# Count groups of one or two nodes with src split 64 x 196 instead of 32 x 391, and group sizes chosen by new tables

## The chip, the cores and the metric

The kernel runs as one program on one core of a Trainium2 chip. The metric is the device time of one execution in microseconds (us), as the median over runs. One execution was also recorded by the hardware profiler; lines such as L920 are lines of the kernel before. The engines are called by the profile's names: PE (TensorE matmul), PEld (its weight load), DVE (VectorE), ACT (ScalarE), POOL (GpSimd) and SP (SyncE, which only issues DMAs).

## What is computed

A graph has 12500 nodes with 64 features and 400000 edges `src -> dst`, sorted by `dst`; `dst` is drawn as 12500 times the square of a uniform number, so nodes with low numbers have many more edges than those with high ones. `src` is uniform. Cut to what matters:

```
x_t  = leaky_relu(x @ W1n + b1n) @ W2n + b2n             # node MLP
e_t  = leaky_relu(ea @ W1e + b1e) @ W2e + b2e            # edge MLP
agg  = segment_sum(x_t[src] * e_t, dst)                  # messages
x    = layernorm(x + layernorm0(x + agg) * gamma + beta) # layer 0
deg  = number of edges with dst = node, plus 1
w    = rsqrt(deg)
h    = x
twice: h = w * (sum over edges (src, dst) of (w*h)[dst] into src  +  w*h)
out  = layernorm(x + h @ W.T + b)                        # layer 1
```

The two hops at the end need, for each pair of nodes, how many edges join them: the count matrix `A[dst, src]`.

## The kernel before

**Three kinds of work share the first 4.3 ms.**

*Messages.* Edges go through in 261 batches `q` of 1536 edges (12 chunks of 128), from the highest `dst` to the lowest. For each chunk POOL issues one indirect DMA (`gathers`, L592) that fetches the 128 rows `x_t[src]` into the tile `xg`; 3125 chunks give 3125 such DMAs. The edge MLP (`hidden`, L624 to L640, and `message`, L648 to L663) runs on PE, ACT and DVE; L659 multiplies by `xg`; `level1` and `level2` (L674 to L720) sum into PSUM by destination, and `nodes` finishes the layer for four windows of 128 nodes at a time. `xg` has four buffers.

*Counting* (`adjacency`, L875). The matrix `A` is made in blocks `k` of four destination nodes, 3125 of them, from the highest to the lowest. `src` is written as `a*391 + b` with 32 values of `a` (`FA`) and 391 of `b` (`FB`). A block's edges are cut into groups of `w` nodes (1, 2 or 4; with w = 8 one group serves two blocks) and a group into slots of at most 128 edges, in a number that depends on the expected count of edges alone (`_plan_slots`, L74). For each slot DVE makes a one-hot matrix of `b` (128 edges x 391, tile `oh`, L910), and for several slots at a time a one-hot of the key `node*32 + a` (tile `koh`, L859, 512 columns wide). One matmul (L920) of the two adds the slot's counts to `w*32` rows of a PSUM bank; with w = 8 there are two matmuls, one for each block. With w = 2 the two groups of a block use halves of 64 rows, with w = 1 four groups use quarters of 32 rows. ACT turns the finished bank into fp8 (`stage`, L935) and every eight blocks one DMA stores them to `adj` in HBM, in runs of 391 bytes. A row of `A` is 32*391 = 12512 columns long (`PITCH`).

The 44 table columns of 128 slots (`NSBP`, a multiple of four) are filled as follows: at the start 44 indirect DMAs (`run`, L320) find where each slot's edges begin, and later one indirect DMA per column (`fetch`, L799) brings the edges. `prepare` (L807, once per four columns, 11 times) computes key and column of every edge on DVE (L814 to L826), and four transposes each on PE spread them.

*First hop* (`hop1`). When a supergroup of rows of `A` has been stored and its nodes are done, PE multiplies it, in 25 pieces of 512 columns (the last of 224), with L1117 and L1129, and `combine` (L1246) adds the result up.

**What sets the order.** The main loop (L1331) has 264 steps `t`. In step `t` it emits the gathers of batch `t+2`, the edge MLP of batch `t`, the messages of `t-1` and so on, and between them as much counting and first hop as a budget says. `_plan_slots` gives each block a cost, `a_total` is their sum with 20 for each block (L1289), and by step `t` the share `(t + lead) / 261` of it is emitted (L1349), with `lead` growing from 1 to 10 over the first 60 steps. So a block's cost decides how many blocks fall into a step. The first hop gets 4400 units a step. The scheduler of the language then orders each engine's queue; the edge work has priority.

A gather also waits for the matmul that `marks` names (L600): the gather that stands nine places back in the queue waits for the matmul that was emitted last. So POOL can't run far ahead of PE.

When all counting is emitted (step 249) the counting buffers are freed, and `scatter_store` (L1083) prepares 27 batches for the second hop. After the last gather the last nodes are finished (L1199 to L1212), and the second hop begins: 24 pieces of 512 columns and one of 224, each with 80 matmuls of 128 rows (L1221) and 80 of 64 (L1232).

## Time and profile before

| | |
|---|---|
| median of 10 runs | 5064.64 us (5056.83 to 5073.96) |
| the profiled execution's own time | 5066.32 us |
| its span, first to last instruction | 5064.5 us |
| mean granted PE clock | 0.904 |
| busy, of the span | PE 86%, PEld 49%, DVE 65%, ACT 45%, POOL 75% |
| gathers (L592) | 3125, 1003 ns each, from 71 us to 4276 us |
| one-hots of columns (L910) | 5556, 334 ns each |
| one-hots of keys (L859) | 1170, about 420 ns each |
| counting matmuls (L920) | 6054 |
| evictions of count banks (L935, L933) | 3125 |

Busy shares say how long an engine had something in work, not whether anything waited for it. What sets the pace has to be read from the waits: an engine whose queue always has an instruction ready, and which starts it as soon as the one before has ended, sets the pace of its stage, whatever its busy share is. In a group's row, the mean is one instruction's own duration; where neighbours overlap, their sum is more than the busy time.

### The profile page before, as it was taken

The page shows a single profiled execution, that of the slowest core. Times are in us where ns is not written, and L with a number is a line of the kernel's source. Part 1 is how long each engine was busy: PE and PEld are TensorE (multiplying, and loading weights), DVE is VectorE, ACT ScalarE, POOL GpSimd, SP SyncE. Part 2 cuts the span into 40 slices and gives each one's busy share as a digit, 9 for nine tenths or more (in the row PEclk, how much of TensorE's full clock was granted, in tenths as well). Part 3 has the DMA queues.
Part 4 walks back from the last instruction along what each step waited for, and adds up shares of the span by engine and source line. Part 5 has one row for each costly group of instructions (what it writes and reads, how often), then busy time and mean ns, then how long its engine had stood idle before and what let it go on. Part 6 is the DMA issues. An engine that isn't in the chain of part 4 may idle for free. (4 is left out here: it accounts for less than half of the span.)

```text
span 5064.5 us, 94143 instructions
## 1 busy us (share of the span) xinstructions
PE 4357.3 (86%) x31344; PEld 2483.7 (49%) x31344; DVE 3267.4 (65%) x11086; ACT 2265.5 (45%) x7868; POOL 3804.5 (75%) x3607
## 2 busy tenths in 40 slices
PE   5776889989989898978897898698787978999997
PEld 3443445545545455544554455354444545444443
DVE  7897778766758786786688686766778856100004
ACT  3887777555545464554555443333332123100003
POOL 6777767777777777777777777777777765688885
PEclk8898999999999798979998899898789967999999
DMA  5998889766768586646674665454333253999998
GB/s 139 182 169 133 142 153 158 146 138 139 144 125 155 116 152 130 127 88 140 136 141 89 132 129 98 86 117 90 65 81 76 66 145 97 231 210 211 205 200 222
DMA packets 1254836, 696.96 MB, mean 138 GB/s; under 512 B 593468, under 2 KB 1188144, under 8 KB 1253312
## 3 DMA queue, kind: packets, MB, share of 16 engines
q1 hardware_dynamic: 1104032, 566.91, 49.1%
q0 software_dynamic: 150304, 123.92, 17.4%
q8 instruction: 248, 4.06, 0.4%
q14 instruction: 252, 2.06, 0.1%
HBM read 494.67 MB, written 195.83 MB: 136 GB/s over the span
## 5 line engine op out<-in xcount | busy, mean ns | idle before, releaser
L592 POOL DMA_INDIRECT xg<-xt_tab,si x3125 | 3134.5, 1003 | 1012.1 <-issue 492.8
L935 ACT ACTIVATE stage<-pa 128x391 fp8e4<-128x391 f32 x3077 | 1514.5, 538 | 1166.6 <-PE pa L920 1089.3
L910 DVE TENSOR_SCALAR oh<-iota_b,colT 128x391 bf16<-128x391 bf16 x5556 | 1605.7, 334 | 188.3 <-PE pa L920 183.5
L920 PE MATMUL pa<-oh,koh 128*128 128x391 bf16 (+2 forms) x6054 | 1303.2, 372 | 279.8 <-ACT stage L935 75.1
L920 PEld LDWEIGHTS <-koh 128*128 128x128 bf16 (+2 forms) x6054 | 607.5, 150 | 664.8 <-issue 371.2
L935 ACT ACTIVATION_READ_ACCUMULATOR stage<-pa 128x1 f32 x3077 | 734.7, 244 | 0.0
L1117 PE MATMUL hacc_p<-at,gp 128*128 128x512 fp8e4 (+1 forms) x2425 | 646.5, 396 | 96.0 <-ACT gp L744 36.6
L659 DVE TENSOR_TENSOR msg<-pe,xg 128x384 f32<-128x384 f32 x522 | 289.8, 555 | 594.0 <-DMA xg<-xt_tab,si 343.8
L1492 POOL DMA_INDIRECT hop_tab<-tot,first x317 | 493.7, 1558 | 100.5 <-issue 93.9
L650 PEld LDWEIGHTS pe<-w,z 128*128 128x128 f32 x3132 | 463.9, 209 | 73.5 <-issue 51.4
L650 PE MATMUL pe<-w,z 128*128 128x128 f32 x3132 | 475.3, 292 | 0.0
L1221 PE MATMUL acc<-at,gp 128*128 128x512 fp8e4 (+1 forms) x2000 | 446.2, 376 | 0.0
L1117 PEld LDWEIGHTS <-gp 128*128 128x128 bf16 x2425 | 231.7, 103 | 406.6 <-issue 162.9
L634 ACT ACTIVATE z<-pw,b1s 128x384 f32<-128x384 f32 x522 | 293.7, 617 | 211.3 <-PE pw L624 203.3
L624 PE MATMUL pw<-eat,w1ab 64*128 64x384 f32 x1044 | 372.5, 601 | 17.7 <-DVE msg L659 12.6
L859 DVE TENSOR_TENSOR koh<-iota_k,keyT 128x512 bf16<-128x512 bf16 (+3 forms) x920 | 384.6, 419 | 0.0
L1129 PE MATMUL hacc_p<-at,gp 128*64 128x512 fp8e4 (+1 forms) x2425 | 367.6, 391 | 0.0
L1600 DVE TENSOR_TENSOR pot<-po,dis 128x256 f32<-128x256 f32 (+2 forms) x26 | 10.5, 408 | 539.4 <-PE po L1594 539.4
L638 DVE SCALAR_TENSOR_TENSOR z<-pw,b,z 128x384 f32<-128x384 f32 x522 | 313.0, 607 | 39.0 <-ACT z L634 35.6
L1221 PEld LDWEIGHTS <-gp 128*128 128x128 bf16 x2000 | 188.2, 99 | 227.4 <-issue 29.0
L684 PE MATMUL pl<-msg,oh 128*32 128x65 f32 x6264 | 170.4, 232 | 127.7 <-DVE msg L659 119.3
L1246 PEld LDWEIGHTS pc<-twoid,hev 128*128 128x128 f32 x1764 | 235.6, 203 | 58.2 <-issue 27.7
(218 smaller groups left out, 3846.2 us busy)
## 6 DMA issues: line engine op xcount, KB each, us to landing
adj<-stage SPq DMA_DIRECT2D x390, 391.0 KB
at<-adj SPq DMA_DIRECT2D x97, 896.0 KB
at<-adj SPq DMA_DIRECT2D x168, 512.0 KB
eat<-in_eaq_dram SPq DMA_DIRECT2D x261, 192.0 KB
xg<-xt_tab,si POOLq DMA_INDIRECT x3125
at<-adj SPq DMA_DIRECT2D x96, 256.0 KB
at<-adj SPq DMA_DIRECT2D x24, 832.0 KB
at<-adj SPq DMA_DIRECT2D x24, 768.0 KB
```

Source lines behind the costliest of these rows:

```text
L592: got = nc.gpsimd.indirect_dma_start(out=xg[:, i, :], out_offset=None, in_=xt_tab, in_offset=bass.IndirectOffsetOnAxis(ap=si[:, c : c + 1] ...
L624: nc.tensor.matmul(pws[h], w1ab[rows, h, :], ea_q[rows], start=True, stop=True, tile_position=(D * h, 0),)
L638: nc.vector.scalar_tensor_tensor(z[:, h, :], pws[h], b1, z[:, h, :], op0=ALU.add, op1=ALU.max)
L650: ended = nc.tensor.matmul(pe[:, :, c, :], z[:, h, c * P : (c + 1) * P], w2, start=False, stop=(c == SCC - 1),)
L859: nc.vector.tensor_tensor(t[:, :, :n], iota_8[:, :, :n] if w == 8 else iota_k[:, : w * FA, :n], keyT[:, None, j0 : j0 + n].to_broadcast([P ...
L910: nc.vector.tensor_scalar(oh, iota_b, colT[:, i % P : i % P + 1], None, op0=ALU.is_equal)
L920: ended = nc.tensor.matmul(to, key, oh, start=(j == 0), stop=(j == caps[g] - 1), tile_position=(0, r0),)
L935: nc.scalar.activation(stage[:, u, :], pa, AF.Identity, saturate=True, accum_out=sums[:, u : u + 1],)
L1117: nc.tensor.matmul(acc[:, :w], gp[:kk, lo + i, 0:2, :].rearrange("p t d -> p (t d)"), t[:kk, i, :w], start=start, stop=False, skip_group_c ...
L1129: nc.tensor.matmul(acc[D * h : D * (h + 1), :w], gp[:kk, lo + i, 2, :], t[:kk, i, :w], start=False, stop=False, skip_group_check=True, til ...
L1221: nc.tensor.matmul(acc[:, :w], gp[:kk, wi, 0:2, :].rearrange("p t d -> p (t d)"), t[:kk, wi - lo, :w], start=first and n == 0, stop=False, ...
L1492: nc.gpsimd.indirect_dma_start(out=hop_tab[(q * QC + i) % HT], out_offset=bass.IndirectOffsetOnAxis(ap=first[:, q - Q0, i : i + 1], axis=0 ...
```

## The change

`FB` becomes 392, `FB2` 196. Groups of one or two nodes (w <= 2, called *halved*) write `src` as `a*196 + b` with 64 values of `a`. Their one-hot of `b` is 196 columns wide, their key is `node*64 + a`, so one slot takes 128 rows with w = 2 and 64 rows with w = 1, and two groups lie side by side in the two halves of a bank's columns. Their slots go group by group instead of by turns, and a dependency keeps their matmuls in that order on PE. A bank is stored in runs of 196 bytes, and a store holds blocks of one kind only. `PITCH` becomes 12544, so the last piece of a hop has 256 columns.

The sizes are chosen by a new table `value`, pairs of blocks with w = 8 are allowed everywhere, and a new table `cost` paces the loop; the empty block of a pair now has the cost 0. `prepare` multiplies by per-slot constants (`sQ`, `sA`, `sF`) where it used constants of the program, and these are made once at the start.

What follows from the two versions of `_plan_slots`, worked out from their formulas:

| | before | after |
|---|---|---|
| slots with w = 1 / 2 / 4 / 8 | 307 / 2389 / 2362 / 498 | 1394 / 2566 / 1401 / 498 |
| slots, counting matmuls | 5556, 6054 | 5859, 6357 |
| one-hots of keys | 1170 | 1425 |
| columns of slots `NSBP` | 44 | 48 |
| `a_total` | 1790922 | 1480492 |
| stores to `adj` | 391 | 394 |

Blocks 2046 and up (w = 4, one slot), 1548 to 2045 (w = 8) and 512 to 1547 (w = 2, two slots) keep their sizes; below 512 most blocks with w = 4 become w = 1.

```diff
-FB = 391
+FB = 392
+FB2 = FB // 2
 PITCH = FA * FB
-PAIR_END = 2304
...
-    cost = {1: 249, 2: 267, 4: 302}
+    cost = {1: 181, 2: 217, 4: 302, 8: 373}
+    value = {1: 51, 2: 61, 4: 82, 8: 109}
...
-            c = cost[w] * sum(caps)
+            c = value[w] * sum(caps)
...
-    for k in range(0, PAIR_END, 2):
+    for k in range(0, NBLK - 1, 2):
...
-        if 2 * n <= sum(blocks[k][2]) + sum(blocks[k + 1][2]):
-            c = cost[4] * n
-            blocks[k], blocks[k + 1] = (c, 8, []), (c, 8, [n])
-    return blocks
+        if value[8] * n < blocks[k][0] + blocks[k + 1][0]:
+            blocks[k], blocks[k + 1] = (0, 8, []), (0, 8, [n])
+    return [(cost[w] * sum(caps), w, caps) for _, w, caps in blocks]
...
+def halved(k):
+
+    return BLOCKS[k][1] <= 2
+TURNS = [4 * k for k in range(NBLK) if halved(k) != (k > 0 and halved(k - 1))]
...
+        with tc.issue_after(mlp_done):
+            nc.vector.memset(sA, 0.0)
+        for u, node in enumerate(TURNS):
+            nc.vector.tensor_scalar(
+                c1, sT, node - 0.5, 1.0 - 2 * (u % 2), op0=ALU.is_gt, op1=ALU.mult
+            )
+            nc.vector.tensor_add(sA, sA, c1)
...
-        nc.vector.tensor_scalar(m, src, 0.5, 1.0 / FB, op0=ALU.add, op1=ALU.mult)
+        nc.vector.tensor_scalar(m, src, 0.5, None, op0=ALU.add)
+        nc.vector.tensor_mul(m, m, sQ[:, ks, None].to_broadcast(wide))
...
-        nc.vector.scalar_tensor_tensor(
-            key, key, float(FA), m, op0=ALU.mult, op1=ALU.add
-        )
+        nc.vector.tensor_mul(key, key, sA[:, ks, None].to_broadcast(wide))
+        nc.vector.tensor_add(key, key, m)
...
-        nc.vector.scalar_tensor_tensor(
-            col, m, -float(FB), src, op0=ALU.mult, op1=ALU.add
-        )
+        nc.vector.tensor_mul(col, m, sF[:, ks, None].to_broadcast(wide))
+        nc.vector.tensor_sub(col, src, col)
...
-        ks = KS // w
+        wk = w if w > 2 else 2 * w
+        ks = KS // wk
...
+            if w <= 2:
+                todo = [(j, g) for g in range(4 // w) for j in range(caps[g])]
...
+                oh = oh[:, : FB2 if w <= 2 else FB]
...
                 else:
-                    rows = slice(g * w * FA, (g + 1) * w * FA)
-                    parts = [(pa[rows, :], rows.start, keys)]
+                    r0 = 0 if w == 2 else g % 2 * 2 * FA
+                    h = g if w == 2 else g // 2
+                    parts = [
+                        (pa[r0 : r0 + 2 * w * FA, h * FB2 : (h + 1) * FB2], r0, keys)
+                    ]
...
+                    if w <= 2 and (j, g) != todo[0]:
+                        behind(mm, ended)
...
+                wide = FB2 if w <= 2 else FB
...
+                    adj[sg][r0 : r0 + 4 * n, :].rearrange(
+                        "(g l) (a b) -> (l a) g b", l=4 * wide // FB, b=wide
                     ),
-                    stage[:, :n, :],
+                    stage[:, :n, :].rearrange("p g (h b) -> p (g h) b", b=wide),
```

## The prediction

> **What bounds the kernel now.** I read the page first. PE is busy for 86% of the span and POOL for 75%, so PE looks like the bound. Then I asked for busy time by stretches; here are four of the quarter-milliseconds:
>
> ```profile
> 250.00:500.00 250.00, 172.14 (x1130) 98.79 (x1124) 209.29 (x794) 209.05 (x845) 187.77 (x189) 0.86 0.88 154
> 1250.00:1500.00 250.00, 227.42 (x1691) 126.61 (x1690) 156.86 (x510) 125.45 (x441) 191.05 (x194) 0.95 0.67 135
> 2250.00:2500.00 250.00, 214.62 (x1539) 124.10 (x1541) 176.57 (x643) 124.69 (x446) 192.20 (x189) 0.91 0.66 134
> 3750.00:4000.00 250.00, 212.71 (x1602) 130.68 (x1602) 202.44 (x678) 64.42 (x144) 192.10 (x191) 0.93 0.36 78
> ```
>
> After the length, the columns are PE, PEld, DVE, ACT and POOL, each with its instruction count, then PE clock, DMA share and GB/s. While the counting changes from groups of eight to four to one, the other columns move, ACT by a factor of three. POOL stays at 191 us and about 192 instructions, whatever the others do. The timeline of POOL says why:
>
> ```profile
> 1202.30 0.94 POOL L592 DMA_INDIRECT xg<-xt_tab,si  x1 [0.30 <-PE pa L920]
> 1203.55 0.94 POOL L592 DMA_INDIRECT xg<-xt_tab,si  x1 [0.30 <-issue]
> 1204.80 0.94 POOL L592 DMA_INDIRECT xg<-xt_tab,si  x1 [0.30 <-PE pa L920]
> ```
>
> Each gather starts 0.30 us after the one before has ended, whatever releaser is named. The waits of POOL alone, from 750 to 4000 us (total, times, longest):
>
> ```profile
> POOL xg L592 <- issue: 394.2, 1293, 0.4
> POOL xg L592 <- PE pa L920: 157.3, 500, 2.1
> POOL xg L592 <- DMA xg<-xt_tab,si: 106.9, 350, 0.5
> POOL xg L592 <- PE pe L650: 18.3, 60, 0.3
> ```
>
> 157.3 us in 500 times is 0.31 us each: that is the fixed gap, not a wait for counting. The other side agrees: from 2000 to 4000 us DVE's L659 waits for gathered rows (143.7 and 145.8 us in the two halves). So from 750 to about 4115 us the gathers set the pace, (1.003 + 0.30) x 12 = 15.6 us a step, and counting runs beside them. It reaches the end only where POOL idles beyond 0.31 us. The timeline has such places early (the longest shown) and after counting:
>
> ```profile
> 614.58 0.94 POOL L592 DMA_INDIRECT xg<-xt_tab,si  x1 [5.17 <-PE pa L920]
> 655.82 0.94 POOL L592 DMA_INDIRECT xg<-xt_tab,si  x1 [3.50 <-PE pa L920]
> 731.21 0.94 POOL L592 DMA_INDIRECT xg<-xt_tab,si  x1 [9.56 <-PE pa L920]
> 4123.54 0.94 POOL L592 DMA_INDIRECT xg<-xt_tab,si  x1 [7.08 <-PE pe L650]
> ```
>
> From 400 to 760 us these excesses sum to 28 us, from 4115 to 4240 us to 22 us, in between to 3.4 us. From the last gather on, the chain of waits is last batch, last nodes, then PE's second hop at one piece per 29.6 us, none of it counting.
>
> **What the change does beside the gathers, worth nothing by itself.** PE: 961 fewer slots of w = 4 by 241 ns (808.8 us / 3358) are 232 us less. Halved slots go from 442.5 + 52.4 = 495 us for 2696 to 3960 at 83 ns (half of the 166 ns from start to start of back-to-back matmuls of 391 columns) to 100 ns (a weight load's busy share, 607.5 us / 6054): 330 to 396 us. In all 330 to 400 us less. DVE: rows of L703 give the slope, (437 - 298) ns for 256 f32 columns; the one-hot's 334 ns less the same fixed part (229 ns) is 0.27 ns a bf16 column, so 196 columns save 52 ns: 3960 x 52 = 206 us less, 303 more slots by 236 ns = 72 us more, 255 more key one-hots by 420 ns = 107 us more, 36 new transforms in `prepare` by 0.6 us and its twelfth call 28 us more. DVE comes out even. ACT's 3125 evictions stay. All this lies under POOL's queue; if that cover were gone, PE's part would be worth up to 400 us and DVE's nothing.
>
> The Trainium skill, TensorEngine Tiling (Array Packing), Key Properties, says tiles of 64 columns run in parallel, which speaks against giving them up. The trace has two counting matmuls of 64 columns starting 0.003 us apart, the next pair 0.165 us later: 83 ns a slot already. By rule and row, w = 2 gains nothing on PE.
>
> **What it puts on the path.** POOL's queue gets eight more indirect DMAs. Four `run` at the start, where POOL goes on without a gap from 10 to 84 us: 4 x (0.94 to 1.08 + 0.30) = 5.2 us, with a larger candidate table in front (792 KB becomes 864, a wait of 8.45 us grows by its share, at most 0.8; 0.5 taken). Four `fetch` among the gathers: 4 x (1.018 + 0.30) = 5.3 us. At the start POOL also waits for the first counting (104.50, idle 4.56 us), which comes after `prepare(0)`: three more transforms of 128x512, 0.43 to 0.69 us, 1.9 us. The 15 small DVE instructions for the constants (0.15 us each) and the twelfth group of the search (1.6 us) lie beside POOL's first gathers, since `fetch` starts at 84.44 without a wait; 3.8 us if that cover is gone. The second hop's last piece has 32 more columns in 80 matmuls and 40 pairs, at 0.42 ns a column (0.2155 us / 512): 1.6 us. Sum of these bills: 14.5 us.
>
> **What it may give back.** *Early stalls, 28 us.* Here blocks of w = 4 with one slot go, 24.5 a step before and 20.3 after (a block costs 322, a step gets `a_total` / 261, 6862 before and 5672 after, times 1.15 while `lead` grows): 0.7 us less for PE (4.2 x 166 ns), 2.1 us less for ACT (4.2 x 0.50 us, from 207 evictions in 104.4 us), a sixth less stored while the DMA share is 0.85 to 0.88. In the trace, the first L659 of a batch comes 10 us after its last gather at batch 24, and 36 us after it at batch 32, where POOL stalls: the slack is about 36 us. Some 0.7 us a step and shorter hiccups keep the backlog near the slack. Bounds 0 and -28; I take -20, as the backlog that overflows is small against the relief over twelve steps.
>
> *The gathers' own duration.* They take 0.94 us at best and 1.003 us on average. I sorted 2899 gathers (200 to 4050 us) by the one-hots L910 that start in their first 0.94 us: none 0.968 us, one 0.992, two 1.021, three 1.018, four 1.174; the slope is 28.6 ns a one-hot, 101 us in all. With a price per start it becomes 5 us more (5859 for 5556); with a price per column 30 us less (3960 at half). The key one-hots add 4 us at 22 ns each by the same fit. Range -30 to +10; I take -10, between the two, since the trace has no one-hot of 196 columns.
>
> The Trainium skill, SBUF — State Buffer, Who interferes with whom, says a DVE instruction in a two-port mode locks GpSimd out for its whole length. The slope agrees in sign; by the rule the price goes with the length, and this term would be near the -30 end.
>
> *The pairs.* The w = 8 stretch goes from 11.0 slots a step to 14.4, 6.8 more matmuls by 166 ns = 1.1 us of PE a step. There PE is busy 577 of 625 us (875 to 1500 us), 14.4 of 15.6 us a step: it becomes 15.5, and there is nothing left to catch up with. The 36 us of slack have to carry the hiccups of 34 steps, for instance DVE's waits for `di` of 31.8 us. Bounds 0 and +32; I take +2, because the stretch begins with a smaller backlog than before.
>
> *Elsewhere.* Steps 240 to 249 cost DVE the same (307 one-hots of columns and 39 of keys before, 345 shorter and 57 after), so the 22 us after counting should return as they are, give or take 8. Stores in runs of 196 bytes: 180000 more packets, in stretches where the DMA share is 0.35 to 0.67; nothing waits there.
>
> **Sum.** 14.5 - 20 - 10 + 2 = -13.5 us against the profiled execution's 5066.3, so 5052.8. It lies 1.7 us over the median; on the median's scale 5051, and I say 5052.
>
> **Rivals.**
> *The pairs' stretch becomes the bound (slower).* Mechanism: in steps 52 to 85 PE needs what a step lasts, the backlog passes 36 us, and `marks` holds the gathers back. It decides once a step takes PE more than 15.6 us. For it: PE's 15.5. Against it: 25.6 such matmuls a step went by at 950 to 1100 us without a stall. Price: 15 us of stall there, early stalls down by only 8, gathers as before: 14.5 + 15 - 8 = +21.5, so 5086.
> *Bills and credits cancel.* Early stalls come from late loads, DVE's wait for `di` at 722 us for one (6.17 us), and stay by half; gathers as before: 14.5 - 14 = 0, 5065.
> *It doesn't do what it says.* DVE isn't relieved at all by my sum, so if anything hangs on DVE it is not lighter. This has the time of the case before.
> *Counting sets the pace after all.* Then PE's 330 us come off in large part; from 5066 this could give 4830. POOL's even gap speaks against it.
>
> **How the numbers follow.** The forecast (gathers keep the pace, early stalls shrink, gathers a little shorter) has 0.60; its own range of 5035 to 5064 reaches past the bound of 0.2% (10 us, about what a measurement of this kernel can tell from no change), 0.47 below it and 0.13 within. The pairs' stretch has 0.27, cancelling (with no relief for DVE) 0.10, counting as the pace 0.03. Faster 0.47 + 0.03 = 0.50, within 0.2% 0.13 + 0.10 = 0.23, slower 0.27. The range goes from all credits at their best (14.5 - 28 - 30 = -43.5, so 5021) to the pairs' rival, 5088.
>
> **What would show it.** In the profile after: gathers still 0.30 us apart from 800 to 4100 us; their mean below 1.003 us; less idle before the gathers at 400 to 760 us; no POOL stall at 900 to 1450 us; the last gather at about 4260 us; the second hop as long as before plus 1.6 us. I am wrong if POOL's idle beyond 0.31 us grows in the pairs' stretch, if the gathers' mean rises, or if the time falls by over 50 us, for then counting did set the pace.

## The result, and the profile after

The change makes the kernel slower: 5115.99 us (median of 9 runs, 5104.17 to 5122.08) against 5065.57 us of the kernel before (31 runs on the same chip), a ratio of 1.0095 [1.0085, 1.0106], some 48 us. The profiled execution spans 5107.1 us against 5064.5. Of the chips that the experiments were run on, four ran the kernel before in 6500 to 6620 us, and two, those of the last two experiments, in 5074 and 5047 us.

The same four stretches as in the prediction, of the kernel after (length; PE, PEld, DVE, ACT, POOL with their instructions; PE clock, DMA share, GB/s):

```profile
250.00:500.00 250.00, 170.27 (x1106) 101.31 (x1106) 187.94 (x707) 187.23 (x742) 190.79 (x190) 0.81 0.66 136
1250.00:1500.00 250.00, 240.85 (x1813) 136.72 (x1812) 186.16 (x620) 150.78 (x547) 190.99 (x192) 0.99 0.69 146
2250.00:2500.00 250.00, 199.96 (x1470) 130.99 (x1470) 165.76 (x673) 122.20 (x435) 183.44 (x188) 0.83 0.94 128
3750.00:4000.00 250.00, 213.34 (x1587) 139.29 (x1586) 189.26 (x725) 67.44 (x162) 191.80 (x192) 0.83 0.45 80
```

POOL holds its 191 us in three of the four. In the third it falls to 183, and there the DMA share has gone from 0.66 to 0.94, with fewer bytes moved (128 GB/s for 134). This is the stretch where groups of two nodes are counted. From 1500 to 2750 us as a whole, first before, then after:

```profile
1500.00:2750.00 1250.00, 1113.43 (x8233) 663.85 (x8232) 961.25 (x3482) 673.67 (x2434) 955.97 (x960) 0.91 0.66 129
1500.00:2750.00 1250.00, 1019.42 (x7939) 655.57 (x7936) 873.88 (x3585) 653.75 (x2341) 911.41 (x919) 0.86 0.97 124
```

The page after shows the added packets in its DMA part (before: 593468 under 512 B, q1 49.1%):

```profile
DMA packets 1435053, 699.06 MB, mean 137 GB/s; under 512 B 773484, under 2 KB 1368160, under 8 KB 1433520
...
q1 hardware_dynamic: 1283920, 568.12, 56.0%
```

The waits of POOL from 1500 to 2750 us (total, times, longest), two lines of before, then three of after:

```profile
POOL xg L592 <- PE pa L920: 68.0, 219, 1.6
POOL xg L592 <- DMA xg<-xt_tab,si: 34.7, 114, 0.3
...
POOL xg L637 <- PE pa L977: 74.6, 194, 3.0
POOL xg L637 <- DMA xg<-xt_tab,si: 55.8, 86, 3.0
POOL xg L637 <- PE pe L695: 10.0, 18, 4.8
```

Before, that is hardly more than the fixed gap of 0.30 us each time. Now 86 waits for an earlier gather's DMA make 55.8 us, of which the gap is 26. The timeline of POOL shows them as single stalls; the last line is one of those after counting:

```profile
1537.99 0.94 POOL L637 DMA_INDIRECT xg<-xt_tab,si  x1 [2.83 <-PE pa L977]
...
1555.14 0.94 POOL L637 DMA_INDIRECT xg<-xt_tab,si  x1 [4.82 <-PE pe L695]
...
1616.80 1.28 POOL L637 DMA_INDIRECT xg<-xt_tab,si  x1 [1.42 <-DMA xg<-xt_tab,si]
...
1838.43 0.94 POOL L637 DMA_INDIRECT xg<-xt_tab,si  x1 [3.04 <-PE pa L977]
...
4138.13 0.94 POOL L637 DMA_INDIRECT xg<-xt_tab,si  x1 [10.61 <-PE pe L695]
```

The names behind the arrows mislead here. POOL's DMAs take eight semaphores in turn, so every gather also waits until the gather eight places ahead has landed. From the trace's semaphore updates I took, for each stall, the time from that landing to the stalled gather's start. Of the 60 stalls over 0.05 us between 1500 and 2750 us, 58 start 0.26 to 0.76 us after it (nearly all 0.74); these 58 hold 56.8 of the 58.3 us of stall. That holds for the 1838.43 line too, which names PE. After counting (4115 to 4330 us) the landing lies 9.9 to 18 us back: those stalls are another thing.

A landing may come up to about 8.7 us after the end of a gather without harm: eight starts at 1.30 us are 10.4, less the gather's own 0.94 and the 0.74. Between 1500 and 2750 us a gather landed 3.14 us after its end (median; 90% within 6.20) before, and 6.23 (9.16) after. So over a tenth of the gathers now lands past that line.

The trace of before had the same thing already, elsewhere: eight of its stalls, 6.8 us in all, start 0.74 to 0.76 us after the landing eight places ahead, and seven of them lie between 180 and 450 us, where the DMA share is 0.94.

Where the span's 42.6 us come from, in POOL's terms (idle beyond 0.31 us ahead of gathers, before and after):

| | before | after | difference |
|---|---|---|---|
| first gather starts | 71.1 | 79.6 | +8.5 |
| four more `fetch` (0.98 + 0.30 each) | | | +5.1 |
| stalls to 400 us | 6.4 | 3.5 | -2.9 |
| stalls 400 to 760 us | 28.0 | 1.7 | -26.3 |
| stalls 760 to 1500 us | 2.1 | 0.8 | -1.3 |
| stalls 1500 to 2750 us | 1.3 | 58.3 | +57.0 |
| stalls 2750 to 4115 us | 0.0 | 2.8 | +2.8 |
| stalls after 4115 us | 21.6 | 36.0 | +14.4 |
| 3125 gathers, mean 1003 and 998 ns | | | -15.9 |
| last gather to the end | 789.4 | 789.7 | +0.3 |

The sum is +41.7 us of the 42.6. (Idle time ahead of `fetch` is not in the table.)

### The profile page after: what moved, and what is told of

It is laid out like the page before. It is cut to its first block, busy times and chain, and to the rows that moved or that the text cites. A ratio compares the mean times of both kernels' runs of the same rounds, so it can differ in the third digit from the quotient of the medians.

```text
span 5107.1 us, 95709 instructions
## 1 busy us (share of the span) xinstructions
PE 4276.0 (84%) x31655; PEld 2553.4 (50%) x31655; DVE 3208.6 (63%) x11710; ACT 2271.1 (44%) x7872; POOL 3796.1 (74%) x3615
## 5 line engine op out<-in xcount | busy, mean ns | idle before, releaser
L996 ACT ACTIVATE stage<-pa 128x392 fp8e4<-128x392 f32 x3077 | 1511.3, 522 | 1103.2 <-PE pa L977 1025.6
L962 DVE TENSOR_SCALAR oh<-iota_b,colT 128x196 bf16<-128x196 bf16 (+1 forms) x5859 | 1469.0, 302 | 240.0 <-PE pa L977 222.4
L977 PE MATMUL pa<-oh,koh 128*128 128x196 bf16 (+2 forms) x6357 | 1155.7, 314 | 290.2 <-DVE msg L704 155.2
L977 PEld LDWEIGHTS <-koh 128*128 128x128 bf16 (+1 forms) x6357 | 631.8, 138 | 676.3 <-issue 457.7
L996 ACT ACTIVATION_READ_ACCUMULATOR stage<-pa 128x1 f32 x3077 | 705.9, 230 | 0.0
L695 PEld LDWEIGHTS pe<-w,z 128*128 128x128 f32 x3132 | 480.7, 215 | 59.4 <-issue 42.3
L905 DVE TENSOR_TENSOR koh<-iota_k,keyT 128x512 bf16<-128x512 bf16 x1175 | 499.4, 427 | 0.0
L669 PE MATMUL pw<-eat,w1ab 64*128 64x384 f32 x1044 | 401.5, 635 | 36.6 <-DVE msg L704 29.7
L729 PE MATMUL pl<-msg,oh 128*32 128x65 f32 x6264 | 187.7, 235 | 210.5 <-DVE msg L704 182.6
L1277 PEld LDWEIGHTS <-gp 128*128 128x128 bf16 x2000 | 188.3, 99 | 227.7 <-issue 28.6
L729 PEld LDWEIGHTS pl<-msg,oh 128*32 128x32 f32 x6264 | 124.8, 115 | 296.6 <-issue 112.4
```

Source lines behind the costliest of these rows:

```text
L669: nc.tensor.matmul(pws[h], w1ab[rows, h, :], ea_q[rows], start=True, stop=True, tile_position=(D * h, 0),)
L695: ended = nc.tensor.matmul(pe[:, :, c, :], z[:, h, c * P : (c + 1) * P], w2, start=False, stop=(c == SCC - 1),)
L905: nc.vector.tensor_tensor(t[:, :, :n], iota_8[:, :, :n] if w == 8 else iota_k[:, : wk * FA, :n], keyT[:, None, j0 : j0 + n].to_broadcast([ ...
L962: nc.vector.tensor_scalar(oh, iota_b[:, : oh.shape[1]], colT[:, i % P : i % P + 1], None, op0=ALU.is_equal)
L977: mm = nc.tensor.matmul(to, key, oh, start=(j == 0), stop=(j == caps[g] - 1), tile_position=(0, r0), skip_group_check=w <= 2,)
L996: nc.scalar.activation(stage[:, u, :], pa, AF.Identity, saturate=True, accum_out=sums[:, u : u + 1],)
```

## The experiments

Three theories. **RUNS**: stores in runs of 196 bytes load the DMA engines, gathers land late, and the wait for the landing eight places ahead stalls POOL. **ORDER**: the new order, sizes and pace of the batches cost the time. **LATE**: TensorE, whose clock in that stretch is 0.86 after and 0.91 before, comes late to its batches and holds POOL back, as the names in the waits say.

### Undo and do alone (eight runs)

`e1_run392`, `r2_run392`: the changed kernel with all stores in runs of 392 bytes; the rows of halved blocks then land in wrong places of `A`, with the same bytes and instructions.

```diff
-                        "(g l) (a b) -> (l a) g b", l=4 * wide // FB, b=wide
+                        "(g l) (a b) -> (l a) g b", l=4, b=FB
                     ),
-                    stage[:, :n, :].rearrange("p g (h b) -> p (g h) b", b=wide),
+                    stage[:, :n, :],
```

`e2_before_split`, `r3_split`: the kernel before, stores of groups of one or two nodes cut in two (196 and 195 bytes; the edit is shortened).

```diff
+                cuts = (0, 196, FB) if all(BLOCKS[first + i][1] <= 2 for i in range(n)) else (0, FB)
+                for c0, c1 in zip(cuts, cuts[1:]):
+                    nc.sync.dma_start(rows[:, :, c0:c1], stage[:, :n, c0:c1])
```

`e3_before_pace`, `r4_pace`: the kernel before, paced by the new cost table. `e4_half1`: the changed kernel with only w = 1 halved. `r1_after`: the changed kernel again.

```diff
+    pace = {1: 181, 2: 217, 4: 302, 8: 373}
+    return [(pace[w] * sum(caps), w, caps) for _, w, caps in blocks]
```

```diff
-    return BLOCKS[k][1] <= 2
+    return BLOCKS[k][1] == 1
```

Expected of the first four:

> The changed kernel with every store to adj in runs of 392 bytes; the rows of halved blocks land in the wrong places of A, all else is as in the changed kernel, same bytes, same instructions. Theory RUNS (180000 more and shorter packets fill the DMA engines where w = 2 blocks are stored, 1500 to 2750 us, so gathers land later and POOL idles between them, 58 us): DMA share there falls from 0.97 to about 0.65, POOL's idle beyond 0.31 us in this stretch from 58 us to under 5, time about 5058. Rival ORDER (the counting matmuls lost their pairs of 64-column tiles and stand in a fixed order, so PE's marks hold the gathers): nothing changes, 5116.

> The kernel before, its stores of blocks with w <= 2 cut in two DMAs of 196 and 195 columns; nothing else. Theory RUNS: DMA share 0.95 in the w = 2 stretch, POOL's idle beyond 0.31 us there 40 to 60 us instead of 1.3, time 5105 to 5125. Rival ORDER: the matmuls are as before, so 5065 (the 130 or so more DMA issues are on SP, which issues little).

> The kernel before with its own groups and forms, but with the loop paced by the changed kernel's cost table (and 0 for the empty block of a pair). Theory PACE (the early stalls went because fewer w = 4 blocks stand in a step): about 21 blocks a step instead of 24.5, POOL's idle beyond 0.31 us from 250 to 1000 us falls from 30 us to under 8, time 5035 to 5043. Rival (the early stalls went for another reason, the row pitch of 392 or the relief of DMA alone): 5060 to 5066.

> The changed kernel, sizes and pace as in it, but only w = 1 halved; w = 2 has its old form (64 rows, 392 columns, by turns), so w = 2 blocks are stored in runs of 392 bytes. Theory RUNS: the stall of 58 us from 1500 to 2750 us is gone, 5055 to 5062. Rival ORDER would say the same for w = 2, so this is read together with the two kernels above; what it adds is the price of halving w = 1 alone, below 512 nodes' blocks: under 5 us of POOL idle from 2750 to 4050 us.

And of the second four, on another chip:

> The changed kernel once more, beside the same runs of the kernel before as the next three. On a chip where the kernel before takes 5065 us (granted clock 0.90), all theories expect 5104 to 5122 us, ratio 1.0095. On a chip that grants a clock of about 0.78 (kernel before 6620 us), TensorE is late to every batch and GpSimd's gathers wait some 0.5 us each for it in both kernels; there the theory RUNS (the 196-byte runs of the stores load the DMA engines and slow the gathers) expects no more than the version of it with 392-byte runs showed on such a chip, ratio 1.014, since nothing that waits for TensorE waits for a gather; the rival ORDER (the new order and sizes of the batches cost the time) expects the same 1.014 there and 1.0095 here.

> The changed kernel with its halved rows stored in runs of 392 bytes, whole partitions as the wide groups' are (the rows of A of groups of one or two nodes land in wrong places, so the result of the hops is wrong; all counts, batches, instructions and bytes stay). Where the kernel before takes 5065 us: RUNS expects the stalls of GpSimd between 1500 and 2750 us to fall from 58 us to under 5 and a time of 5055 to 5070 us; ORDER expects 5110 to 5120 us and the stalls unchanged. On a chip with clock 0.78: both expect no difference from the changed kernel, within 15 us.

> The kernel before with each store of a group of one or two nodes cut into two DMAs of 196 and 195 columns: the short runs alone, with the old order, sizes and 391-column counting. Where the kernel before takes 5065 us: RUNS expects a DMA share of about 0.95 between 1500 and 2750 us, stalls of GpSimd of 20 to 70 us there, and 5085 to 5130 us; ORDER expects 5060 to 5070 us. On a chip with clock 0.78 it was measured at a ratio of 0.998 to the kernel before.

> The kernel before with the changed kernel's cost table used for the pace alone (blocks, sizes, widths and stores stay). Where the kernel before takes 5065 us: if the early stalls of GpSimd (22 us between 500 and 750 us) go with the pace, 5035 to 5045 us and under 3 us of stall there; if they go with the cheaper one-hots, 5060 to 5070 us. On a chip with clock 0.78 it was measured at a ratio of 1.0086.

Measured, as ratios to the kernel before on the same chip (6620.3 us for e1 to e4, 6506.5 for r1 to r4):

| | ratio | DMA share 1500 to 2750 us | 90% of gathers land within, us |
|---|---|---|---|
| e1_run392 | 1.0141 [1.0106, 1.0175] | 0.42 | |
| e2_before_split | 0.998 [0.996, 0.9999] | 0.55 | |
| e3_before_pace | 1.0086 [1.0059, 1.0113] | 0.43 | |
| e4_half1 | 1.0205 [1.0166, 1.0244] | 0.41 | |
| r1_after | 1.0232 [1.0188, 1.0276] | 0.59 | 6.82 |
| r2_run392 | 1.019 [1.0153, 1.0227] | 0.45 | 4.82 |
| r3_split | 0.9993 [0.9971, 1.0014] | 0.63 | 7.29 |
| r4_pace | 1.0114 [1.0064, 1.0165] | 0.46 | 5.10 |

The first four expectations failed together, since none had foreseen a chip on which gathers don't set the pace: they start 1.85 us apart there. The first line below is `r1_after`, the second `r2_run392`, both from 1500 to 2750 us:

```profile
1500.00:2750.00 1250.00, 977.94 (x6269) 573.56 (x6268) 677.22 (x2491) 515.46 (x1844) 694.74 (x699) 0.80 0.59 103
```

```profile
1500.00:2750.00 1250.00, 985.95 (x6323) 577.94 (x6324) 680.16 (x2506) 515.91 (x1846) 689.68 (x698) 0.80 0.45 103
```

POOL starts 699 instructions in the time in which it started 919 on the first chip, and the length of the runs changes that by one. But the share falls from 0.59 to 0.45, a packet of the stores takes 26.1 ns where one of half the length takes 31.5, and a gather's 2048-byte packet takes 177 ns for 196. In `r3_split`, the kernel before with the cut, the share is 0.63 and a gather's packet takes 214 ns; in `r4_pace`, without the cut, 0.46 and 188. The first half of RUNS, that short runs load the DMA engines and slow the gathers' packets, is shown in both directions; whether late landings stall POOL could not be seen where POOL waits for TensorE anyway. The last column is to be read with care: on these four chips only 23 to 35% of the semaphore updates of POOL's DMAs are on record (98% on the first chip), so a landing may be later than the last update that is there. Packets and instructions are complete.

The changed kernel's 1.9 to 2.3% on this chip (1.4% was expected) are for the most part not the runs' but the order's, the sizes' or the pace's (the pace alone has 1.1%): ORDER holds there, and says nothing on the 48 us.

### Why these chips are slow, and TensorE lightened (eight runs)

Two timelines side by side, first `r1_after`, then the kernel before on the first chip:

```profile
1019.21 0.55 PE L729 MATMUL pl<-msg,oh 128*32 128x65 f32 x24
...
1026.32 0.21 ACT L738 COPY tot<-pl 128x65 f32<-128x65 f32 x1 [4.78 <-remote]
```

```profile
2007.76 0.55 PE L684 MATMUL pl<-msg,oh 128*32 128x65 f32 x24
...
2008.38 0.22 ACT L693 COPY tot<-pl 128x65 f32<-128x65 f32 x1 [1.42 <-PE pl L684]
```

The copy that waits for the matmuls starts 6.6 us after their last record in `r1_after` and 0.07 us after it on the first chip. From 750 to 4000 us the median of this delay is 0.12 us before on the first chip and 5.8 us in `r3_split`. In the records PE's semaphore updates stop for some microseconds and then come in a burst, with most engines waiting. That the engines stand still is shown by the times of their instructions. That the updates themselves come late is not, since 16% of PE's updates and 36% of DVE's have no record in `r1_after` (1% on the first chip).

`l1_before` to `l4_split` take work off TensorE, so that its lateness should no longer count; `u1_before` to `u4_split` also replace the 32-column matmuls of `level1`. Each set has the kernel before, the changed kernel, and the 392-byte and cut stores of above (edits shortened).

```diff
             for i in range(i0, i1):
                 hm(i, first and i == 0)
-            for i in range(i0, i1):
-                lw(i)
...
+            hm(i0, first and i0 == 0)          # in place of both loops
...
-            for c in range(SCC):               # message
+            # only c = 0
...
-                for s in range(4):             # level1, u1 to u4 only
-                    nc.tensor.matmul(pl[REL * s : REL * (s + 1), :], ..., tile_position=(0, REL * s))
+                nc.tensor.matmul(pl, oh[:, 4 * c : 4 * c + 4, :].rearrange("p q r -> p (q r)"), m[:, 4 * c, :], ...)
```

> The kernel before, lightened on TensorE: of each batch of up to 16 matmuls of the first hop only the first runs, and of the three matmuls of 128 columns that add the edge MLP's second layer (`message`) only the first (so the hop and two thirds of the messages are wrong; all loads, stores, gathers, evictions and all counting stay). On the traced stretch from 1500 to 2750 us this takes some 320 us of the hop's 373 and 95 of the second layer's 143 off 1113 us of TensorE. If the low clock alone (TensorE late to every batch) made the 6500 to 6620 us on these chips, GpSimd's gathers set the pace again: 1.30 us from start to start, last gather at 4200 to 4300 us, 5000 to 5100 us in all. If another cause slows these chips, the gathers keep their 1.85 us.

> The changed kernel with the same matmuls left out. If the gathers set the pace again, its time stands to the lightened kernel before as the changed kernel to the kernel before in the first result: RUNS (short runs of the stores load the DMA engines) expects stalls of GpSimd of 30 to 70 us where groups of two are stored and 30 to 60 us more than the lightened kernel before. The rival LATE (TensorE, held back to a clock of 0.86 there against 0.91, came late to the batches, and so the gathers stalled) expects no stalls now that TensorE has 40% less to do, and a time within 15 us of the lightened kernel before.

> The lightened changed kernel with stores in runs of 392 bytes (halved rows land in wrong places). RUNS: stalls under 5 us where groups of two are stored, 35 to 60 us less than the lightened changed kernel. LATE and ORDER: as the lightened changed kernel, within 10 us.

> The lightened kernel before with each store of a group of one or two nodes cut into two DMAs of 196 and 195 columns. RUNS: a DMA share over 0.85 there, stalls of 15 to 60 us, 15 to 60 us more than the lightened kernel before. LATE and ORDER: as the lightened kernel before, within 10 us.

> The kernel before, lightened on TensorE as before (one matmul in sixteen of the first hop, one in three of the edge MLP's second layer) and with `level1`'s twelve f32 matmuls in 32-column tiles replaced by three whole ones (sums of the wrong chunks; loads, stores, gathers, evictions and all counting stay). On the chips of these runs `tot` starts 5.8 us (median) after the last record of those matmuls, on the first chip 0.12 us. Theory TILES: that wait of some 6 us a batch, 261 times, is what makes 6500 to 6620 us of 5065; without it GpSimd's gathers set the pace again, 1.30 us from start to start, last gather at 4250 to 4320 us, 5030 to 5100 us in all. If the wait moves to another matmul, the gathers keep 1.8 us and the time stays over 6000 us.

> The changed kernel with the same left out and replaced. If the gathers set the pace again: RUNS (short runs of the stores load the DMA engines and slow the gathers) expects a DMA share of 0.85 to 1 between 1500 and 2750 us, 30 to 70 us of GpSimd stalls there and 20 to 60 us more than the kernel before so changed. LATE (TensorE at a low clock was late to its batches) expects under 5 us of stalls, as TensorE has 40% less to do, and a time within 15 us of the kernel before so changed.

> The same of the changed kernel, with all stores in runs of 392 bytes (halved rows land in wrong places). RUNS: DMA share 0.6 to 0.7 and stalls under 5 us between 1500 and 2750 us, 30 to 60 us less than with the short runs. LATE and ORDER (the new order and sizes of the batches cost the time): as with the short runs, within 10 us.

> The same of the kernel before, with each store of a group of one or two nodes cut into two DMAs of 196 and 195 columns. RUNS: DMA share over 0.85 between 1500 and 2750 us, stalls of 15 to 60 us there, 15 to 60 us more than without the cut. LATE and ORDER: as without, within 10 us.

| | us (kernel before there) | DMA share 1500 to 2750 us | 90% of gathers land within, us |
|---|---|---|---|
| l1_before | 6449.4 (6611.2) | 0.43 | 4.22 |
| l2_after | 6627.4 | 0.55 | 5.98 |
| l3_run392 | 6599.8 | 0.42 | 4.15 |
| l4_split | 6469.9 | 0.56 | 5.39 |
| u1_before | 6155.8 (6514.8) | 0.43 | 3.99 |
| u2_after | 6248.7 | 0.55 | 5.92 |
| u3_run392 | 6248.8 | 0.42 | 4.03 |
| u4_split | 6183.8 | 0.56 | 5.22 |

The gathers' pace did not come back, and TILES, that the wait behind the 32-column matmuls makes these chips slow, falls: without the 32-column matmuls `tot` follows after 0.20 us, but the time is 5.5% less, not 22%, and POOL still stalls, behind other matmuls. Less work makes TensorE idle more, and the granted clock falls with it, from 0.785 to 0.697 in `l1_before`. The Trainium skill, TensorE: Matmul & The Clock Gate, Part 1, says that an idle TensorE is put at half rate; the trace agrees. (In `l1_before` the granted clock is either full or half, and half for 3912 of the 6441 us.) What holds these chips back stays open.

All eight runs show RUNS' first half once more: a share of 0.55 or 0.56 with short runs, 0.42 or 0.43 with long ones. In time nothing clear follows. Long runs took 28 us off `l2_after` and nothing off `u2_after`; the cut added 20 us to `l1_before` and 28 us to `u1_before`, with spreads that overlap. `l2_after` and `u2_after` are 178 and 93 us slower than the kernels before that are lightened in the same way, where RUNS expected 20 to 60 and LATE under 15: on these chips most of the change's price is ORDER's or that of something untested.

### Gathers, stores and loads by themselves

`b1_alone` has no TensorE at all (the code is shortened). POOL issues gathers back to back, SyncE issues `eat` loads, stores and 512-byte loads at the traced rates, each released by a gather's landing.

```diff
+    for b in range(nb):                        # 14 stages of 12 batches
+        after_gather(nc.sync.dma_start(eat, eaq[b]).ins)
+        for i in range(QC):
+            got.append(nc.gpsimd.indirect_dma_start(out=xg[:, i, :], in_=xpad, ...).ins)
+            if pos in at_pos:                  # (0, 8, 16) of 24
+                after_gather(nc.sync.dma_start(adj[r0 : r0 + 32, :].rearrange(
+                    "(g l) (a b) -> (l a) g b", l=4 * wide // FB, b=wide), stage).ins)
+            if at and (pos == 4 or (pos == 17 and b // 2 % 2)):
+                after_gather(nc.sync.dma_start(at, rows[...]).ins)    # 14x128 runs of 512 bytes
```

> A kernel of its own: no TensorE, no counting, no layers (its output is the input rows). GpSimd issues 14 stages of 144 gathers like L637 back to back, and SyncE loads `eat` beside them; a DMA or one-hot is released by the landing of the gather five places back, so the loads keep step with the gathers. Stages: gathers alone; stores of eight blocks in runs of 392 bytes, three in 24 gathers, with loads of 14x128 runs of 512 bytes, three in 48 gathers (the rates of the stretch with groups of two); the same in runs of 196; both once more; 196 without the 512-byte loads; twice as many stores, 392 and 196; runs of 98; then gathers with two one-hots of 392 columns each, two of 196, four of 196; and both store forms with their one-hots. Every gather waits for the landing of the one eight places back. RUNS: gathers alone, and with runs of 392, go at 1.24 to 1.26 us from start to start with less than 1 us of stall a stage; with runs of 196 a gather lands in 5 us or more (median; 3 with 392) and the stage has 3 to 15 us of stall; 392 twice as often costs about what 196 does, since both have 2048 packets where one has 1024; 98 and 196 twice hold GpSimd for 20 us or more a stage. LATE and ORDER: no stage with stores has stalls beyond 1 us, since without TensorE nothing comes late. One-hots: gathers of 0.94 us rise by 0.02 to 0.03 us for each one-hot of 392 columns, by under 0.012 for each of 196.

On a chip where the kernel before takes 5074 us. Stretches of the stages without stores, with 392, with 196, with 392 twice as often and with 196 twice as often (length; DVE, POOL; PE clock, DMA share, GB/s):

```profile
18.00:182.00 164.00, 10.48 (x11) 124.00 (x132) 1.00 0.23 50
198.00:362.00 164.00, 10.48 (x11) 124.07 (x132) 1.00 0.55 125
378.00:545.00 167.00, 10.48 (x11) 123.70 (x132) 1.00 0.91 116
...
1111.00:1275.00 164.00, 10.48 (x11) 124.07 (x132) 1.00 0.81 163
1291.00:1491.00 200.00, 10.48 (x11) 123.67 (x132) 1.00 1.26 121
```

The same 132 gathers take 164 us beside long runs and 167 to 200 beside short ones, each gather still 0.94 us. (A share is the packets' summed time, and may pass 1.) The stalls of the first 196-byte stage, in its timeline:

```profile
381.04 0.94 POOL L2434 DMA_INDIRECT xg<-in_xpad_dram,si  x1 [1.29 <-DMA xg<-in_xpad_dram,si]
...
424.80 0.94 POOL L2434 DMA_INDIRECT xg<-in_xpad_dram,si  x1 [1.63 <-DMA xg<-in_xpad_dram,si]
...
488.27 0.94 POOL L2434 DMA_INDIRECT xg<-in_xpad_dram,si  x1 [1.36 <-DMA xg<-in_xpad_dram,si]
```

| stage (132 gathers each) | stall, us | landing, median and 90%, us | ns a store packet |
|---|---|---|---|
| gathers alone | 0.0 | 1.51, 1.71 | |
| 392, and again | 0.0, 0.0 | 2.06, 4.37; 2.21, 4.47 | 24.2, 24.7 |
| 196, and again | 3.4, 6.7 | 4.99, 8.07; 5.21, 8.86 | 33.2, 32.9 |
| 196 without the 512-byte loads | 2.2 | 3.99, 6.93 | 31.7 |
| 392 twice as often | 0.0 | 4.15, 6.00 | 29.1 |
| 196 twice as often | 36.3 | 9.58, 11.92 | 46.1 |
| 98 | 51.2 | 10.02, 12.89 | 40.7 |
| 392 and 196 with their one-hots | 0.0, 4.9 | 2.04, 4.35; 4.90, 8.22 | 24.3, 33.5 |

RUNS' second half is shown: without TensorE, short runs alone stall the gathers, and each stalled gather starts 0.26 us (median) after the landing eight places ahead. LATE falls: the stalls come without TensorE, and in the kernel 58 of 60 follow a landing. 3.4 to 6.7 us for 132 gathers would be 24 to 46 us for the 914 of the stretch (an estimate); the kernel has 58, with more kinds of transfer beside. What was not done is to run the changed kernel with long runs on a chip where the gathers set the pace, so its 48 us are explained by these two halves, not undone. One part of the expectation fell: 392 twice as often, with as many packets as 196 and twice the bytes, costs nothing. It isn't the number of packets alone.

The one-hots, in stages without stores: a gather takes 0.943 us alone, 0.956 beside two of 392 columns, 0.945 beside two and 0.948 beside four of 196. That is 6.5 and 1 ns a one-hot; the longer was expected at 20 to 30.

### What makes a short packet dear

`b2_runs` keeps the stages and changes the store's run, or the distance from run to run in memory.

```diff
+                # shortened: the run in one piece; each store waits for a gather as above
+                to = adj[r0 : r0 + 32, :].rearrange("(g l) (a b) -> (l a) g b", l=l, b=dist)
+                nc.sync.dma_start(to[:, :, :run], stage[:, :n, :run])
```

> Again without TensorE and counting (the output is the input rows): gathers back to back with `eat`, stores and loads as in the stages above, three stores in 24 gathers, 512-byte loads beside them, twelve stages with another form of the store's runs each (stages of 144 gathers, 24 gathers without stores between them). In the stages above one packet of 392 bytes took 24.2 ns, one of 196 bytes 33.2 ns, though the few 196-byte packets that ran after the rest of a stage was done took 16.0. COUNT (twice as many packets keep the engines busier, whatever they hold): runs of 192, 196, 200 and 256 bytes, next to each other or apart, take 28 to 36 ns a packet each, hold gathers up alike (3 to 10 us of stall a stage), and only 384, 391 and 392 are at 24 and free of stalls. NEIGHBOUR (short runs that lie next to each other without filling whole aligned pieces of memory hinder each other): 196 and 200 side by side take 30 to 36 ns and stall; 196 at distances of 256 or 392, and 192 and 256, take 15 to 24 ns, a DMA share under 0.75, no stall; of the pair 196 + 195 bytes the second takes over 40. Loads in runs of 1024 bytes in place of 512 (half as many packets of them) take some 0.1 off the DMA share beside the 196-byte runs and about half of the stall.

196 side by side, 196 at a distance of 256, 192 side by side, 196 at a distance of 392, and 196 with loads of 1024 bytes (columns as above):

```profile
228.00:396.00 168.00, 10.48 (x11) 124.37 (x132) 1.00 0.93 116
441.00:605.00 164.00, 10.48 (x11) 123.90 (x132) 1.00 0.58 124
651.00:815.00 164.00, 10.48 (x11) 124.08 (x132) 1.00 0.53 123
...
1281.00:1449.00 168.00, 10.48 (x11) 123.13 (x131) 1.00 0.90 116
...
1926.00:2091.00 165.00, 10.48 (x11) 123.75 (x132) 1.00 0.90 118
```

| run, bytes (distance) | ns a packet | stall, us | | run, bytes (distance) | ns a packet | stall, us |
|---|---|---|---|---|---|---|
| 392 (392) | 27.2 | 0.0 | | 256 (256) | 17.8 | 0.0 |
| 391 (391) | 26.9 | 0.0 | | 200 (200) | 28.0 | 2.0 |
| 384 (384) | 22.8 | 0.0 | | 196 (196) | 33.2 | 3.6 |
| 192 (192) | 15.0 | 0.0 | | 196 (392) | 32.4 | 5.0 |
| 192 (256) | 15.0 | 0.0 | | 196 + 195 (391) | 17.0, 52.5 | 8.6 |
| 196 (256) | 16.2 | 0.0 | | 196, loads of 1024 | 33.5 | 1.3 |

COUNT (only the number of packets matters) falls: 192 and 256 bytes come in as many packets and cost half. NEIGHBOUR (a run is dear for touching the next) falls in its form: runs of 196 at a distance of 392 touch nothing and cost 32.4 ns. What is left is where the runs start: at multiples of 192 or 256 a short packet takes 15 to 18 ns on average, at multiples of 196 or 200 it takes 28 to 33. Multiples of 192 are multiples of 64 but not all of 128, so for 192 bytes 64 is enough; runs of 200 start at multiples of 8, which is not. What lies between was not tried.

These means hide which packets are dear. The table has the packets of a store in the order of their start, in eighths of the store (ns a packet, mean over the stores that stand apart from others):

| run (distance), packets in a store | 1st | 2nd | 3rd | 4th | 5th | 6th | 7th | 8th |
|---|---|---|---|---|---|---|---|---|
| 196 (196), 2048 | 16 | 16 | 16 | 16 | 17 | 30 | 79 | 60 |
| 196 (256), 2048 | 16 | 16 | 16 | 16 | 16 | 16 | 16 | 18 |
| 196 (392), 2048 | 16 | 16 | 16 | 17 | 18 | 25 | 77 | 74 |
| 196, then 195 (391), 1024 each | 16 | 16 | 17 | 17 | 18 | 44 | 75 | 71 |
| 391 (391), 1024 | 24 | 24 | 24 | 24 | 24 | 25 | 27 | 44 |
| 196 (196) in the changed kernel, 1500 to 2750 us, 2048 | 16 | 16 | 17 | 17 | 19 | 34 | 80 | 60 |

A packet of 196 bytes at multiples of 196 is as cheap as one at multiples of 256 in the first five eighths of its store, and four to five times as dear in the last two. The pair splits for the same reason: its 195-byte halves come second. So the price of a store may hang on its length as well as on its starts, and a store of half as many blocks might be cheap; that was not tried, nor is it shown what fills up. It also leaves open whether 392 bytes stall nothing for their length or because such a store has only 1024 packets.

Loads with half the packets take more than half of the stall away, but only 0.03 off the share.

## Why the prediction was wrong

**The step that failed** is the half sentence on the stores: "180000 more packets, in stretches where the DMA share is 0.35 to 0.67; nothing waits there". Both halves were wrong. The share did not stay: 250880 packets at the old 31.1 ns in place of 130048 are 0.19 more share, which the trace of before could have told; they took 36.1 ns on average, the packets beside them grew too (512 bytes from 36.9 to 40.9 ns, a gather's 2048 from 223 to 253), and it became 0.97. And something did wait: the line `POOL xg L592 <- DMA xg<-xt_tab,si: 106.9, 350, 0.5`, shown in the prediction and read as the fixed gap, names a wait of a gather for an earlier one. At 0.31 us each it cost nothing, because the landing was there with time to spare; the step never asked how much. This one zero was worth +60 us (57.0 and 2.8; of the 2.8, 1.9 follow a landing). No rival contained it; the slower one had put its mechanism into the stretch of the pairs.

The Trainium skill, DMA: Bandwidth & Descriptors, Specifications, has a rule that would have spoken against the change: transfers under 512 bytes are read-modify-write. By itself it tells nothing of this size, since 391 bytes were under it already, and `b2_runs` shows 192-byte runs at 15.0 ns without a stall.

**Bills**, +14.5: measured 15.3. The first gather starts 8.5 us later (5.7 predicted), `fetch` has 5.1, POOL idles 1.4 longer in its two waits ahead of the first counting (0.65 and 4.56 us before, 2.81 and 3.83 after; 1.9 predicted), the end has 0.3 for 1.6. Right in sum, with misses that largely cancel.

**Early stalls**, -20 with -28 as the bound: -26.3 from 400 to 760 us. Right, on the good side, though not all by the mechanism predicted: 4.4 of the 28.0 us were stalls on a landing, not a backlog that overflows. Whether the new pace or the relief took them away is not shown: `r4_pace` ran where POOL stalls throughout.

**The gathers' duration**, -10: -15.9. Right. The reason fits in direction: one-hots of 196 columns hardly disturb a gather in `b1_alone`, but 392 columns cost 6.5 ns there for the fit's 28.6, so most of that fit must be something else that falls in the same places; what, was not tested.

**The pairs' stretch**, +2 within 0 to 32: -1.3. The first rival did not happen; PE has 240.85 us in the last quarter-millisecond of it, and the one stall there, 0.8 us, follows a landing.

**The stalls after counting**, 0 with 8 either way: +14.4. Outside; these name PE's `pe` and no landing is near. Their cause was not tested.

**The gathers set the pace**, and counting lies hidden behind them: right. PE's busy time fell by 81 us in the whole, and the time rose. (The work beside the gathers was mis-sized: 330 to 400 us less were predicted for PE, and the counting matmuls' own busy time fell by 148 us; DVE's fell by 59 where it was to come out even. Neither sets the pace here.)

The terms that were argued out sum to -28 (15.3 - 26.3 - 15.9 - 1.3), where -13.5 was predicted; with them alone the time would have been some 5038 us, inside the range. The zero and the tail, 60 and 14, turned that into a rise.

## What to carry to other kernels

A wait that costs nothing is a wait with slack, and its slack is a number to be worked out: here eight places of 1.30 us against a landing of 3 to 6. Ask of every transfer that a change adds what else lands later for it, even in stretches where the share is far from 1. Before a store's rows are cut in half, look where the runs will start: 192 bytes at multiples of 192 took less than half the time of 196 at multiples of 196, and the dear ones were the last of a long store. And a releaser's name in a profile is a guess; semaphore times settle it, if the trace has them: count the updates on record first.

## What the runs showed of the hardware that was not expected

- A store packet of 196 bytes takes longer on average (33 ns) than one of 392 (24 to 27), unless it starts at a multiple of 256 (16.2). Of a store of 2048 side by side, the first five eighths take 16 to 17 ns a packet, the last two 79 and 60. Twice as many stores of 392 bytes stalled nothing.
- A gather blocked on the landing eight places ahead starts 0.74 us after it in the kernel and 0.26 us (median) in `b1_alone`.
- Four of the chips ran the kernel before in 6500 to 6620 us. Instructions that wait for TensorE start late there (`tot` by 5.8 us in the median, 0.12 on the first chip), and most semaphore updates of POOL's DMAs are missing from the trace; dense stages did not suffer (from the last gather to the end 800 us in `r3_split`, 789 on the first chip). With part of TensorE's work left out (an estimated 415 of 1113 us between 1500 and 2750 us, by the rows of before) they were 2.4% faster, with the 32-column matmuls gone too 5.5%. The cause stays open.
- No version was found that beats both. The pace table alone on the kernel before, which costs 0.9 to 1.1% on the slow chips, and stores whose runs start at multiples of 64 or more bytes are untried where the gathers set the pace.
